# A message-passing layer on one core: three small moves in the order of work

## The chip, the cores and the metric

The kernel runs on one core of a Trainium2 chip. The metric is the device time of one execution in microseconds (us). Before the change the median of three runs is 1985.5 us (1981.94 to 1990.43). A separate execution was taken with the hardware profiler: 1976.44 us, of which 1974.5 us lie between the program's first and last instruction (the span). All views of the profile come from that one.

Engines: TensorE (PE, with its weight loads shown apart as PEld), VectorE (DVE), ScalarE (ACT), GpSimd (POOL) and SyncE (SP). SP, ACT and POOL also issue the DMAs, each on a queue of its own; an issuing instruction on SP or ACT is shown as SPq or ACTq.

## The reference

A graph has 12,500 nodes with 64 features each and 200,000 edges, sorted by target node. In short:

```python
nodes = x[edges].reshape(E, 128)                  # source row, target row
gates = ssp(edge_attr @ We1 + be1) @ We2 + be2    # ssp(v) = softplus(v) - log 2
gates = gates * (1 - sigmoid(5 * (dist - 3.5)))
h = ssp(nodes @ Wn1 + bn1) @ Wn2 + bn2
message_sum = zeros.at[edges[:, 1]].add(h * gates)
new = x + (ssp(message_sum @ Ws1 + bs1) @ Ws2 + bs2)
out = layernorm(x + new)
```

## The kernel before

**Groups and steps.** The edges are cut into 391 groups of 512, each of two halves of 256, and each half into two chunks of 128, so a group has four chunks. A loop over steps i (from -3, line 628) works on several groups at once: it transposes group i+3, runs layer 1 of group i+1, layer 2 of group i-1 and the scatter of group i-3. The order of instructions is written out by hand; each engine executes its own part of it in that order.

**What a group needs.** Source rows are gathered from x by POOL, one indirect DMA per chunk of 128 rows (line 230, tile xg), 14 groups ahead of the step, into 18 buffers. 40 chunks of all are instead fetched row by row with plain DMAs (line 250, tile xr), 17 of them on SP's queue and 23 on ACT's; `fetch` reads four scaled row numbers (a row number times 256 bytes) into registers first (line 244, tile rows_i). Edge features come by one SP transfer per group (line 268, tile eT, 128 partitions of 256 numbers, 7 buffers). Since the edges are sorted, the targets of a half lie in a window of 42 nodes. A table in DRAM holds, for each node, the target's part of layer 1; two SP transfers per group (line 275, tile wns) bring the windows of 42 table rows, with bases read into registers for two groups at a time (line 270). The chunk's one-hot of the target in its window is made by DVE (line 282).

**One step on PE**, in order: layer 2's bias into the PSUM tile gh (line 338, a product of three bf16 pieces, 512 columns), layer 2 of the edge features (342), layer 1's bias into the PSUM tile z (305, 256 columns), layer 1 of the edge features (307), layer 1 of the nodes (313, rows of xT against wns), the scatter (365), four transposes (296), and layer 2 of the nodes (348). There are two buffers each of z, gh and the transposes' tile. All waits of a step on transfers and on the one-hot are gathered on its first instruction, line 338, through `behind`; the list is

```python
needs = [("xcopy", i + 1), ("load", i + 1)]
needs += [(name, g) for g in ahead[i] for name in ("gather", "onehot")]
```

ACT then does the exponential (324), the logarithm (327) and the copy of the transposes (301); DVE does softplus (332), the products h and msg (357, 361) and the adding of windows into sums (382). About every 15 steps the sums of 512 nodes are complete and a node block (layers on the sums and the layer norm, lines 398 to 461) is strewn over the following steps. From step 380 on, the last ten groups run in a shorter pipeline (`ends`).

**The start.** Constants, indices and x are loaded; SP's queue carries, in this order, src_i, dst_h, three of seven parts of xT, rows_i, dist (tile cut), dst_l (tile rel), and later the other four parts of xT. ACT's queue carries the constants, Wn1 copied 14 times into wns (448 KB), then low_d, base_b, row_d and rows. low_d and base_b take the smallest target of each half through DRAM to all partitions; row_d and rows do the same for the biases in bf16 pieces (line 563, 565). ACT's next work behind them is copying the table's products from PSUM (578). DVE's first instruction is the scaling of the row numbers (492). After that the table stage (line 571 on) computes the table in 14 slices: PE multiplies, ACT and DVE copy, SP writes it to DRAM. Gathers of groups 5 to 13 are issued between the slices, each behind a small memset on DVE (223).

**DMA semaphores.** SP's and ACT's transfers (those of `fetch` aside) share eight semaphores, dealt out in turn in the order in which the program is laid down; a transfer waits until the last one on its semaphore has landed.

Of the kernel before, what the change touches and what calls it, by code (L numbers as in the profile page):

```python
# [42 lines left out]
F32 = mybir.dt.float32  # L43
# [4 lines left out]
OP = mybir.AluOpType  # L48
# [9 lines left out]
P = 128  # L58
D = 64
HE = 256  # L60
# [61 lines left out]
def gnn_resnorm_kernel(ctx: ExitStack, tc: tile.TileContext, a: dict, out: bass.AP, E: int):  # L122
    nc = tc.nc
    x = a["x"]
    N = x.shape[0]
    NG = a["eT"].shape[1]
# [12 lines left out]
    loads = ctx.enter_context(tc.tile_pool(name="loads", bufs=LOADS + 2))  # L139
# [3 lines left out]
    def z_tile():  # L143
        return psum.tile([P, 2, NB], F32, name="z")
# [34 lines left out]
    ones3 = const.tile([PIECES, HE], BF16, name="ones3")  # L179
    be3 = const.tile([PIECES, 2, D], BF16, name="be3")  # L180
    row3 = const.tile([PIECES, 2, K, D], BF16, name="row3")
# [3 lines left out]
    xgs, xrs, eTs = {}, {}, {}  # L185
    made = {}

    def note(key, ins):
        made.setdefault(key, []).append(ins)
        return ins  # L190

    def behind(ins, *keys):

        for key in keys:
            for other in made.get(key, []):
                tc.add_manual_dep(ins.ins, other.ins.name,
                                  mybir.DependencyInfo(mybir.DependencyClass.Sync, mybir.DependencyReason.DATA),
                                  reason="one place of a step takes its waits")
# [64 lines left out]
    bases = {}  # L263

    def load(g):
        eTs[g] = loads.tile([P, HE], F32, name="eT")
        old = ("scatter", g - LOADS - 2 - 4)
        behind(note(("load", g), nc.sync.dma_start(eTs[g], a["eT"][:, g, :])), old)  # L268
        if g % 2 == 0:
            _, at = nc.values_load_multi_w_load_instructions(  # L270
                base_i[32:33, 2 * g : 2 * g + 4], engines=[SP], min_val=0, max_val=8 * D * (N - 1),
                skip_runtime_bounds_check_because="they were clamped to these bounds")
            bases[g], bases[g + 1] = at[:2], at[2:]
        for h in range(2):
            behind(note(("load", g), nc.sync.dma_start(  # L275
                wns[D:DW, g % REST, h, :].bitcast(U8),
                table_bytes[:, bass.ds(bases[g][h], 8 * D * W)].rearrange("o (w f) -> (o w) f", w=W))), old)
# [21 lines left out]
    def xcopy(g):  # L299
        xT = work.tile([DW, K, P], F32, name="xT", bufs=3)  # L300
        note(("xcopy", g), nc.scalar.copy(xT, xTs[g]))  # L301
        xTs[g] = xT.rearrange("f (t h) e -> f h t e", h=2)

    def layer1_edge(g):
        nc.tensor.matmul(zs[g][:, 0, :HE], be3.rearrange("q h d -> q (h d)"), ones3, start=True, stop=False,  # L305
                         skip_group_check=True)
        nc.tensor.matmul(zs[g][:, 0, :HE], we1.rearrange("a h d -> a (h d)"), eTs[g], start=False, stop=True,  # L307
                         skip_group_check=True)

# [22 lines left out]
        nc.vector.scalar_tensor_tensor(ss[g].rearrange("p i t e -> p (i t e)")[:, part], us[g][:, part], BIG,  # L332
                                       z_of(g)[:, part], OP.min, OP.max)

    def layer2_edge(g, *needs):
        gh = gh_tile()
        v = gh.rearrange("p (i t h d) -> p i t h d", i=2, t=2, h=2)
        first = nc.tensor.matmul(gh, ones3[:, :P], row3.rearrange("q i k d -> q (i k d)"), start=True, stop=False,  # L338
                                 skip_group_check=True)
        behind(first, *needs)  # L340
        for t in range(2):
            nc.tensor.matmul(v[:, 0, t], ss[g][:, 0, t, :], we2, start=False, stop=False, skip_group_check=True)  # L342
        ghs[g] = gh.rearrange("p (i k d) -> p i k d", i=2, k=K)
# [128 lines left out]
    with tc.manual_schedule():  # L472
# [4 lines left out]
        with tc.tile_pool(name="prep", bufs=1) as prep:  # L477
# [11 lines left out]
            for i in range(3):  # L489
                load_x(i)  # L490
            nc.sync.dma_start(rows_i, a["rows"])
            nc.vector.tensor_scalar(rows_i, rows_i, float(4 * D), None, OP.mult)
            dist = cut.rearrange("p g k -> p (g k)")
            nc.sync.dma_start(dist, a["dist_l"])
            dst_i = rel.bitcast(I32)
# [75 lines left out]
            for i in range(PARTS):  # L571
                for c in range(i * CP, (i + 1) * CP, CP // 2):
                    m = CP // 2
                    ps = z_tile().rearrange("p b (k f) -> p (b k) f", k=K)
                    for k in range(m):
                        nc.tensor.matmul(ps[:, k, :], xT[:, c + k, :], wnb, start=True, stop=True)
                    tb = prep.tile([P, m, 2 * D], F32, name="tb", bufs=6)
                    nc.scalar.copy(tb[:, :K, :], ps[:, :K, :])
                    nc.vector.tensor_copy(tb[:, K:, :], ps[:, K:m, :])
                    nc.sync.dma_start(by_node[:, c : c + m], tb)  # L580
                    nc.vector.memset(sums[:, c * P : WIDE if c + m == NCH else (c + m) * P], 0.0)
                    for g in waiting.get(c // m, []):
                        gather(g, after=True)
                if i == 1:
                    nc.vector.tensor_copy(base_i[:1], base_b[:1])
                    nc.vector.tensor_scalar(base_i[32:33], base_b[32:33], float(8 * D), None, OP.mult)
                    for k in range(2):
                        nc.vector.tensor_copy(be3[:, k, :], rows[:, 0, :])
                    for k in range(K):
                        nc.vector.tensor_copy(row3[:, :, k, :], rows[:, 1:3, :])  # L590
                        nc.vector.tensor_copy(rs3[:, k, :], rows[:, 3, :])
                if i == 2:
                    nc.vector.tensor_scalar(dist, dist, CUTOFF - 1.5, 5.0, OP.subtract, OP.mult)
                    nc.scalar.activation(dist, dist, AF.Sigmoid)
                    nc.scalar.preload_act_table_set("natural_log_exp_and_others")
                    nc.vector.tensor_scalar(dist, dist, -1.0, 1.0, OP.mult, OP.add)
                    nc.vector.tensor_copy(rel, dst_i)
                    for t in range(2):
                        r = rel[:, :, 2 * t : 2 * t + 2]
                        nc.vector.tensor_sub(r, r, base_b[:, :NH].rearrange("p (g h) -> p g h", h=2))  # L600


        with tc.tile_pool(name="finish", bufs=1) as finish:
# [24 lines left out]
            for i in range(-3, last - 1):  # L628
# [7 lines left out]
                if i < ends:  # L636
                    needs = [("xcopy", i + 1), ("load", i + 1)]
                    needs += [(name, g) for g in ahead[i] for name in ("gather", "onehot")]
                    for g in second[i]:
                        layer2_edge(g, *needs)  # L640
                    if i >= -1:
                        zs[i + 1] = z_tile()
                        layer1_edge(i + 1)
                        for part in early:
                            part.tensor(tx_tile())
                    if i >= -1:
                        layer1_node(i + 1)
                    for n, g in enumerate(third[i]):
                        scatter(g, zs[i + 1][:, 1, HE + 2 * W * n : HE + 2 * W * (n + 1)])
                    at(exps, i + 1)  # L650
                    fetch(i, 1, 0, 0, ROWS // 2)
                    at(logs, i + 1)
                    fetch(i, 1, 0, ROWS // 2, ROWS // 2)
                    for g in ahead[i]:
                        transposes(g)
                        xcopy(g)
                    fetch(i, 1, 1)
                    for g in second[i]:
                        layer2_node(g)
                    for g in second[i]:  # L660
                        hcut(g)
                        message(g)
                    for g in third[i]:
                        window(g)
                    for part in early:
                        part.others()
                    at(softplus, i + 1)
                else:
                    for g in ahead[i]:
                        transposes(g)  # L670
                        xcopy(g)
                    zs[i + 1] = z_tile()
                    layer1_edge(i + 1)
                    for part in early:
                        part.tensor(zs[i + 1][:, 1, HE:])
                    layer1_node(i + 1)
                    exps(i + 1)
                    logs(i + 1)
                    for g in second[i]:
                        layer2(g)  # L680
                        hcut(g)
                        message(g)
                    softplus(i + 1)
                    for g in third[i]:
                        scatter(g, tx_tile()[:, : 2 * W])
                        window(g)
                    for part in early:
                        part.others()
# [19 lines left out]
            begun.pop(2).others()  # L708
            transposes(last)
            xcopy(last)  # L710
            zs[last] = z_tile()
            layer1_edge(last)
            layer1_node(last)
            for some in (edge, node):
# [177 lines left out]
```

## Time and profile before

| | |
|---|---|
| profiled execution | 1976.44 us, span 1974.5 us |
| median of three runs | 1985.5 us |
| PE busy | 1845.7 us (93%) |
| DVE busy | 1086.9 us (55%) |
| ACT busy | 922.5 us (47%) |
| POOL busy | 1447.6 us (73%), 1523 gathers |
| DMA engines, mean busy share in the loop | 0.28 |
| mean granted TensorE clock | 0.976 |

How to read the lines shown: in groups of instructions, a line has the source line, engine, operation, tile written <- tiles read, count | busy time in us, mean ns of one | idle time of the engine before them in us, and what ended it. In the timeline the columns are start, duration (us), engine, line, operation, tiles and count, and in brackets the idle time just before with what released the engine. In the tables by windows the columns are the window, its length, busy time and count on each engine, the granted clock, the DMA engines' busy share and GB/s. Matmuls are pipelined and their ends are modelled, so a busy PE need not be at its peak.

### The profile page before, as it was taken

The page shows a single profiled execution, that of the slowest core. Times are in us where ns is not written, and L with a number is a line of the kernel's source. Part 1 is how long each engine was busy: PE and PEld are TensorE (multiplying, and loading weights), DVE is VectorE, ACT ScalarE, POOL GpSimd, SP SyncE. Part 2 cuts the span into 40 slices and gives each one's busy share as a digit, 9 for nine tenths or more (in the row PEclk, how much of TensorE's full clock was granted, in tenths as well). Part 3 has the DMA queues.
Part 4 walks back from the last instruction along what each step waited for, and adds up shares of the span by engine and source line. Part 5 has one row for each costly group of instructions (what it writes and reads, how often), then busy time and mean ns, then how long its engine had stood idle before and what let it go on. Part 6 is the DMA issues. An engine that isn't in the chain of part 4 may idle for free.

```text
span 1974.5 us, 46877 instructions
## 1 busy us (share of the span) xinstructions
PE 1845.7 (93%) x11373; PEld 1532.7 (78%) x11373; DVE 1086.9 (55%) x2774; ACT 922.5 (47%) x1318; POOL 1447.6 (73%) x1527
## 2 busy tenths in 40 slices
PE   2899998999999999999999999999999999999996
PEld 2788877877777887778788787777877777878875
DVE  2555555555554565555555555565556555655664
ACT  0355544544444554444454544455444444544543
POOL 5777777777777777777777777777777777777771
PEclk9999999999998999999999999999999999999998
DMA  7422222222222222222222222222222323222320
GB/s 208 149 64 67 65 66 66 66 66 66 68 65 69 68 67 67 66 66 68 70 64 70 70 66 70 66 72 71 69 71 65 71 70 72 69 70 68 95 67 14
DMA packets 177321, 143.47 MB, mean 73 GB/s; under 512 B 53193, under 2 KB 149661, under 8 KB 177044
## 3 DMA queue, kind: packets, MB, share of 16 engines
q1 hardware_dynamic: 121052, 88.13, 15.5%
q0 software_dynamic: 48736, 50.00, 13.2%
q10 hardware_dynamic: 7256, 2.27, 0.6%
q8 instruction: 97, 1.59, 0.3%
q14 instruction: 180, 1.47, 0.3%
HBM read 130.59 MB, written 9.63 MB: 71 GB/s over the span
## 4 chain that ended last, share of the span: by engine, by line
PE 49%; SPq 30%; issue 9%; DMA 4%; DVE 2%; POOL 2%; ACTq 2%; ACT 1%; DVEq 0%; POOLq 0%
SPq L250 12%; PE z L313 10%; PE gh L348 8%; PE z L307 7%; PE gh L342 7%; SPq L275 6%; SPq L244 6%; PE tx L296 4%; PE z L365 4%; PE gh L338 3%; SPq L268 3%; POOL xg L230 2%; PE z L305 2%; SPq L270 2%; DMA wns<-table 2%
## 5 line engine op out<-in xcount | busy, mean ns | idle before, releaser
L230 POOL DMA_INDIRECT xg<-in_x,src_i x1523 | 1447.4, 950 | 483.8 <-issue 363.1
L324 ACT ACTIVATE u<-z 128x768 f32<-128x768 f32 x392 | 315.9, 806 | 626.6 <-PE z L365 417.9
L357 DVE TENSOR_TENSOR h<-gh,cut 128x256 f32<-128x256 f32 x391 | 165.9, 424 | 593.5 <-PE gh L348 577.2
L327 ACT ACTIVATE u<-u,one 128x768 f32<-128x768 f32 x392 | 365.9, 933 | 236.1 <-ACT u L324 229.2
L313 PE MATMUL z<-xT,wns 106*128 106x256 f32 x1564 | 419.9, 392 | 0.0
L332 DVE SCALAR_TENSOR_TENSOR s<-u,z 128x768 f32<-128x768 f32 x392 | 372.6, 951 | 77.4 <-ACT u L327 67.0
L348 PE MATMUL gh<-consts,s 128*128 128x64 f32 x3128 | 394.9, 270 | 0.0
L348 PEld LDWEIGHTS gh<-consts,s 128*128 128x128 f32 x3128 | 383.4, 193 | 0.1
L313 PEld LDWEIGHTS z<-xT,wns 106*128 106x128 f32 x1564 | 305.3, 197 | 46.3 <-ACT xT L301 0.9
L307 PE MATMUL z<-eT,consts 128*128 128x256 f32 x782 | 281.2, 442 | 0.0
L342 PE MATMUL gh<-consts,s 128*128 128x128 f32 x1564 | 280.7, 302 | 0.0
L342 PEld LDWEIGHTS gh<-consts,s 128*128 128x128 f32 x1564 | 205.6, 191 | 90.7 <-issue 89.9
L365 PEld LDWEIGHTS z<-xg,msg 128*128 128x128 f32 x1512 | 236.7, 198 | 22.2
L296 PE MATMUL tx<-consts,xg 128*106 128x128 f32 x1524 | 238.0, 277 | 4.0 <-DVE xg L282 2.7
L301 ACT COPY xT<-tx 106x512 f32<-106x512 f32 x391 | 221.6, 567 | 13.2 <-PE tx L296 13.0
L382 DVE TENSOR_TENSOR sums<-sums,z 64x42 f32 x756 | 148.7, 197 | 137.6 <-issue 56.2
L365 PE MATMUL z<-xg,msg 128*128 128x84 f32 x1512 | 223.0, 271 | 0.0
L338 PE MATMUL gh<-row,ones 3*128 3x512 bf16 x391 | 148.9, 381 | 71.8 <-DMA wns<-table 46.6
L296 PEld LDWEIGHTS tx<-consts,xg 128*106 128x106 f32 x1524 | 181.5, 144 | 5.1 <-DVE xg L282 3.0
L361 DVE TENSOR_TENSOR msg<-gh,h 128x256 f32<-128x256 f32 x391 | 165.8, 424 | 13.4
L307 PEld LDWEIGHTS z<-eT,consts 128*128 128x128 f32 x782 | 119.1, 192 | 47.8 <-issue 2.0
L282 DVE TENSOR_TENSOR xg<-consts,rel 128x168 f32<-128x168 f32 x391 | 128.7, 330 | 0.1
(103 smaller groups left out, 604.1 us busy)
## 6 DMA issues: line engine op xcount, KB each, us to landing
eT<-in_eT SPq DMA_DIRECT2D x391, 128.0 KB
xr<-in_x ACTq DMA_DIRECT2D x2944, 0.2 KB
xr<-in_x SPq DMA_DIRECT2D x2176, 0.2 KB
xg<-in_x,src_i POOLq DMA_INDIRECT x1523
wns<-table SPq DMA_DIRECT2D x782, 21.0 KB
table<-tb SPq DMA_DIRECT2D x14, 448.0 KB
sums<-in_xT SPq DMA_DIRECT2D x7, 455.0 KB
y<-in_x SPq DMA_DIRECT2D x24, 128.0 KB
```

The costliest lines, as they stand in the source:

```text
L230: note(("gather", g), nc.gpsimd.indirect_dma_start(out=xg[:, k, :D], out_offset=None, in_=x, in_offset=bass.IndirectOffsetOnAxis(ap=src_i[ ...
L250: ins = queues[queue].dma_start(row_tiles[n, "in"][r + j : r + j + 1, :D].bitcast(U8), x_bytes[:, bass.ds(row_at[queue][j], 4 * D)])
L296: nc.tensor.transpose(tx[:, k, :], xgs[g][:, k, :DW], ident)
L301: note(("xcopy", g), nc.scalar.copy(xT, xTs[g]))
L307: nc.tensor.matmul(zs[g][:, 0, :HE], we1.rearrange("a h d -> a (h d)"), eTs[g], start=False, stop=True, skip_group_check=True)
L313: nc.tensor.matmul(zn, wns[:, g % REST, h, :], xTs[g][:, h], start=True, stop=True, skip_group_check=True)
L324: nc.scalar.activation(us[g][:, part], z_of(g)[:, part], AF.Exp)
L327: nc.scalar.activation(us[g][:, part], us[g][:, part], AF.Ln, bias=one)
L332: nc.vector.scalar_tensor_tensor(ss[g].rearrange("p i t e -> p (i t e)")[:, part], us[g][:, part], BIG, z_of(g)[:, part], OP.min, OP.max)
L342: nc.tensor.matmul(v[:, 0, t], ss[g][:, 0, t, :], we2, start=False, stop=False, skip_group_check=True)
L348: nc.tensor.matmul(ghs[g][:, 1, 2 * t + h, :], ss[g][:, 1 + h, t, :], wn2, start=False, stop=h == 1 and t == 1, skip_group_check=True)
L365: ins = nc.tensor.matmul(sc, msgs[g][:, 2 * t : 2 * t + 2, :].rearrange("p h f -> p (h f)"), xgs[g][:, 2 * t : 2 * t + 2, D:DW], start=t = ...
```

## The change

Three things move. Layer 1's bias product is taken out of `layer1_edge` into `layer1_bias`; in the steps before the last ten it is issued first in the step, ahead of layer 2's bias, and takes the step's waits with it. Edge features of two groups come in one transfer, issued for the even one, into a tile of twice the size with four buffers. The scaling of the row numbers leaves the start of DVE's work and goes into the second part of the table stage.

```diff
     def load(g):
-        eTs[g] = loads.tile([P, HE], F32, name="eT")
         old = ("scatter", g - LOADS - 2 - 4)
-        behind(note(("load", g), nc.sync.dma_start(eTs[g], a["eT"][:, g, :])), old)
         if g % 2 == 0:
+            n = min(2, NG - g)
+            both = loads.tile([P, 2, HE], F32, name="eT", bufs=4)
+            behind(note(("load", g), nc.sync.dma_start(both[:, :n], a["eT"][:, g : g + n, :])), old)
+            for j in range(n):
+                eTs[g + j] = both[:, j]
             _, at = nc.values_load_multi_w_load_instructions(
...
+    def layer1_bias(g, *needs):
+        zs[g] = z_tile()
+        first = nc.tensor.matmul(zs[g][:, 0, :HE], be3.rearrange("q h d -> q (h d)"), ones3, start=True, stop=False,
+                                 skip_group_check=True)
+        behind(first, *needs)
+
     def layer1_edge(g):
-        nc.tensor.matmul(zs[g][:, 0, :HE], be3.rearrange("q h d -> q (h d)"), ones3, start=True, stop=False,
-                         skip_group_check=True)
...
-    def layer2_edge(g, *needs):
+    def layer2_edge(g):
...
-        first = nc.tensor.matmul(gh, ones3[:, :P], row3.rearrange("q i k d -> q (i k d)"), start=True, stop=False,
-                                 skip_group_check=True)
-        behind(first, *needs)
+        nc.tensor.matmul(gh, ones3[:, :P], row3.rearrange("q i k d -> q (i k d)"), start=True, stop=False,
+                         skip_group_check=True)
...
             nc.sync.dma_start(rows_i, a["rows"])
-            nc.vector.tensor_scalar(rows_i, rows_i, float(4 * D), None, OP.mult)
...
                     nc.vector.tensor_scalar(base_i[32:33], base_b[32:33], float(8 * D), None, OP.mult)
+                    nc.vector.tensor_scalar(rows_i, rows_i, float(4 * D), None, OP.mult)
...
+                    if i >= -1:
+                        layer1_bias(i + 1, *needs)
                     for g in second[i]:
-                        layer2_edge(g, *needs)
+                        layer2_edge(g)
                     if i >= -1:
-                        zs[i + 1] = z_tile()
                         layer1_edge(i + 1)
```

In the last ten steps `layer1_bias` stands directly ahead of `layer1_edge`, as the product did before.

More of the change, by code (lines that the diff above doesn't have):

```diff
@@ L671, in gnn_resnorm_kernel @@
                         xcopy(g)
-                    zs[i + 1] = z_tile()
+                    layer1_bias(i + 1)
                     layer1_edge(i + 1)
@@ L710, in gnn_resnorm_kernel @@
             xcopy(last)
-            zs[last] = z_tile()
+            layer1_bias(last)
             layer1_edge(last)
```

## The prediction

> **What bounds the kernel now.** I read the page first, then how far the gathers run ahead of PE (counts of two lines over growing windows), then SP's timeline in mid-run, the timeline of the first 45 us, and the last 80 us.
>
> The page's totals mislead: PE looks like the bound, POOL idle for a quarter of the time.
>
> ```profile
> PE 1845.7 (93%) x11373; PEld 1532.7 (78%) x11373; DVE 1086.9 (55%) x2774; ACT 922.5 (47%) x1318; POOL 1447.6 (73%) x1527
> L230 POOL DMA_INDIRECT xg<-in_x,src_i x1523 | 1447.4, 950 | 483.8 <-issue 363.1
> ```
>
> The idle time before a gather is "issue": 0.30 us after each, so a gather costs 0.95 + 0.30 = 1.25 us. 1523 of them are 1904 us, 4.87 us per group (391 groups). POOL waited for something only at the start (2.85 and 13.85 us), and it issues its last gather at 1930.75 us.
>
> Gathers issued (first fence) and layer 2 bias products, L338, one per step (second fence), from the start to 200, 1000 and 1895 us:
>
> ```profile
> 0.00:200.00 200.00, 137.11 (x142) 1.00 0.45 121
> 0.00:1000.00 1000.00, 742.29 (x780) 0.98 0.31 78
> 0.00:1895.00 1895.00, 1419.56 (x1494) 0.98 0.30 74
> ```
> ```profile
> 0.00:200.00 200.00, 9.39 (x25) 2.26 (x25) 1.00 0.45 121
> 0.00:1000.00 1000.00, 73.39 (x193) 17.50 (x193) 0.98 0.31 78
> 0.00:1895.00 1895.00, 143.87 (x378) 34.26 (x378) 0.98 0.30 74
> ```
>
> A group takes four gathers less the 40 chunks that SP and ACT fetch by rows (2, 20 and 40 of them by then), and step i needs group i+3. So at 200 us POOL has finished 36 groups and step 25 needs the 29th, a lead of 7; at 1000 us 200 against 197, a lead of 3; at 1895 us 383 against 382, a lead of 1. PE takes less per step than POOL, and its margin is used up just at the end. Group 382 (counting from 0) is gathered last at 1891.72; a gather lands 2.42 us after its start (chain of waits), at 1894.1; step 379, which needs it, starts at 1895.06. That is 0.9 us of room, and from there to the end PE is dense for 79 us.
>
> In mid-run PE is paced by SP's queue, two steps of which are:
>
> ```profile
> 499.85 1.24 SPq L250 DMA_DIRECT2D xr<-in_x  x4
> 501.19 0.37 SPq L268 DMA_DIRECT2D eT<-in_eT  x1
> 501.65 0.85 SPq L275 DMA_DIRECT2D wns<-table  x2
> 503.22 3.20 SPq L250 DMA_DIRECT2D xr<-in_x  x8
> 506.52 0.37 SPq L268 DMA_DIRECT2D eT<-in_eT  x1
> 507.54 0.78 SPq L275 DMA_DIRECT2D wns<-table  x2
> ```
>
> From 499.85 to the next such row at 509.09 is 9.24 us, 4.62 per step; the gaps between the rows are loads of bases and row numbers into registers (L270, L244), not waits. A node block's transfers come on top. PE idles before L338 for 71.8 us in all, 46.6 of them put down to wns. The chain names POOL around 240 to 340 us, but there POOL leads by about 6 groups: that is an attribution, not a limit.
>
> The start, timeline and waits:
>
> ```profile
> 20.43 0.22 DVE L492 TENSOR_SCALAR rows_i<-rows_i 40x128 int32<-40x128 int32 x1 [20.43 <-DMA rows_i<-in_rows]
> 25.00 0.30 ACTq L526 DMA_DIRECT2D low_d<-lowT  x1
> 26.21 1.57 SPq L487 DMA_DIRECT2D sums<-in_xT  x4
> 27.00 0.36 ACTq L528 DMA_DIRECT2D base_b<-low_d  x1
> 31.64 0.24 ACTq L563 DMA_DIRECT2D row_d<-pieces  x1
> 39.44 0.26 ACTq L565 DMA_DIRECT2D rows<-row_d  x1
> 43.09 0.06 DVE L223 MEMSET xg<- 128x1 f32 x1
> 43.42 0.94 POOL L230 DMA_INDIRECT xg<-in_x,src_i  x1 [13.85 <-DVE xg L223]
> ```
>
> DVE stands still for 20.43 us before the scaling of the row numbers, and all that follows on it waits: the bases (25.00), their round trip through DRAM, and at the end ACT, which can't copy the table's first products before row_d has landed (39.44). POOL's 13.85 us hang on that copy.
>
> **The change, part by part.**
>
> *Row numbers scaled later.* DVE's first wait becomes dst_h, issued at 1.70, ahead of rows_i (4.02). By 10 us the queues had moved 2.7 MB and dst_h ends at 1.7 MB of SP's, so I take about 9.5 us; the bounds are 4 and 16 us and matter little. DVE's chain from there to low_d (20.89 to 25.00, 4.1 us) then ends near 14, and the pieces near 20.5. But low_d goes out on ACT's queue behind wns (448 KB, issued 2.18, landed 26.2: SP's wait of 14.9 us on it ends at 26.21). A small transfer behind a large one on ACT's queue waits: row_d, 1.5 KB, took 7.8 us behind base_b. So the new limit is wns. The built order of the changed kernel shows that dist and rel (782 KB each) no longer compete with it: the eight DMA semaphores are dealt out in another order, dist now waits for wns, xT's sixth part for base_b. In the 6 us from 18 to 24 us, 289 GB/s moved 1.7 MB, nearly the size of those two, so wns could land at 20 at best, at 26.2 at worst; its rest is slow small packets, and I take 22.5. From wns's landing to base_b's issue is 0.8 us (26.21 to 27.00) and from there to row_d's landing 12.4 us (27.00 to 39.44), now beside dist and rel and two parts of xT rather than four parts: 8 to 14 us, kept at 12.4. Row_d lands at 22.5 + 0.8 + 12.4 = 35.7, **3.7 us earlier** (bounds 28.8 and 41.0: 10.6 earlier, 1.6 later). ACT's copies, L223 and POOL's restart move by the same. The multiply itself, 0.22 us, now stands before a tb copy on DVE: at most 0.2 us of PE's table stage, behind which POOL no longer waits. The first reader of the row numbers is ACT at 93.5 us.
>
> *Edge features in pairs.* 391 transfers become 196. Each removed one frees SP of its issue and wait, 0.46 us (501.19 to 501.65): SP's two steps shrink from 9.24 to 8.8 us, 4.4 per step. The 256 KB land in one piece, one step earlier than needed for the odd group; the queue rests at a DMA share of 0.28. Behind the removed wait comes the next: PE's own step, from the chain 0.32 + 0.64 + 0.21 + 0.63 + 0.86 + 0.41 + 0.44 + 0.85 = 4.36 us, with node blocks (about 2 us, 25 times) 4.49. Both are under POOL's 4.87. So PE eats its lead sooner and then waits for gathers, about 0.4 us a step. The gain here is the room at step 379: **0.9 us** (0 to 1).
>
> *Layer 1's bias first.* The same instructions in another order: L305 (0.21 us) goes ahead of L338 and L342. It carries the step's waits, plus z's release by softplus of two steps before. On DVE that softplus (L332) stands before the one-hot (L282), and a step waits for this one anyway, so nothing new ends last. Weight loads may overlap worse or better, 0.1 us a step either way; the 0.4 us of waiting for gathers covers it. Without that cover it would be 391 x 0.1 = 39 us. I take 0.
>
> Sum: 3.7 + 0.9 = 4.6 us off the profiled execution, from 1976.4 (span 1974.5 and 2 around it) to 1971.8. The median shown, 1985.5, lies 9.1 above that execution. If the surplus is late PE or SP work, the new slack swallows it; if it is slower gathers, none. I give a third, 3 us: 1985.5 - 4.6 - 3 = **1978**.
>
> [...] By stretches of 100 us the granted clock lay between 0.93 and 1.00, though PE idled at the fronts of steps by up to 2.7 us. [...]
>
> **Rivals.**
>
> 1. *The start does not move* (base_b slower beside dist and rel, or wns late). For it: all share the same 16 engines, at a share near 1.0 from 10 to 24 us. Against: 1.6 MB less beside wns. Then 0 to 4 us less than before: 1981 to 1985.
> 2. *POOL is no limit*, and SP's relief comes through: 46.6 to 71.8 us of PE's idle time go, 1985.5 - 4 - 47 to 72, so 1910 to 1934. Against it: 80 gathers in each 100 us, all run long.
> 3. *Slower: the wait at the front costs PE its clock.* PE's 4.49 us per step grow past POOL's 4.87 once the mean clock falls under 4.49/4.87 = 0.92. At 0.90 a step takes 4.99, and over the second 195 steps 0.12 x 195 = 23 us are lost: 2001. For it: the granted clock was 0.93 from 600 to 700 us, where PE had waited 1.7 us for wns (612.61, chain of waits). Against: the new waits are short and regular.
>
> **How the numbers follow.** Forecast 0.74 (times 1970 to 1986, by the bounds of the start and of the surplus), rival 1 0.12, rival 2 0.04, rival 3 0.10. The range 1968 to 1987 takes in the forecast and rival 1, less the far ends of the start, and leaves out the others. This kernel's runs can tell 0.5% from no change, 9.9 us. Faster than 1975.6: four tenths of the forecast, 0.29, and rival 2: 0.33. Slower than 1995.4: 0.09 of rival 3. Between: 0.58.
>
> **What would show it.** DVE's first wait ends by 12 us; the first copy of the table and POOL's restart near 39.5 instead of 43.4; SP's transfers of eT 196, with SP at times idle; L338's wait on wns nearly gone, and L305 now waiting for gathers; POOL still 80 gathers per 100 us, last one near 1927; the last gather to the end 43 us as before. The prediction is wrong if POOL's spacing changes, if wns still lands at 26, or if PE's clock falls under 0.92.

## The result and the profile after

The changed kernel takes 1968.63 us (median of five runs, 1964.49 to 1973.58) against 1985.71 (median of five, 1981.94 to 1990.43) for the kernel before: ratio 0.9915, 95% interval 0.9891 to 0.9939, 17.1 us less. The profiled execution takes 1968.45 us, of which 1966.5 are the span: 8.0 us less than before's profiled execution. The two are not of one kind: the changed kernel's is one of its five timed runs, before's is none of its five and lies 5.5 us under the fastest of them.

The page's busy times with its lines of the gathers and of the step's first product, now layer 1's bias (L309). Then, from tables by windows, the gathers counted from the start to 200, 1000 and 1888 us, and the products of L309, one per step, to 200 and 1888 (L309 works for group i+1, from step -1 on, so 29 of them is step 27, and 381 is step 379):

```profile
PE 1750.5 (89%) x11373; PEld 1491.4 (76%) x11373; DVE 1077.2 (55%) x2774; ACT 922.5 (47%) x1318; POOL 1445.0 (73%) x1527
L230 POOL DMA_INDIRECT xg<-in_x,src_i x1523 | 1444.8, 949 | 475.3 <-issue 319.4 <-DMA xg<-in_x,src_i 67.1 <-PE tx L299 31.1
L309 PE MATMUL z<-ones,be 3*128 3x256 bf16 x391 | 105.3, 269 | 167.8 <-DMA wns<-table 64.9 <-PE gh L354 29.2 <-DMA xg<-in_x,src_i 21.2
```
```profile
0.00:200.00 200.00, 143.37 (x148) 1.00 0.45 126
0.00:1000.00 1000.00, 748.32 (x788) 0.98 0.30 80
0.00:1888.00 1888.00, 1420.09 (x1497) 0.97 0.29 75
...
0.00:200.00 200.00, 7.79 (x29) 2.63 (x29) 1.00 0.45 126
...
0.00:1888.00 1888.00, 102.32 (x381) 34.52 (x381) 0.97 0.29 75
```

PE reaches step 27 by 200 us where it had reached step 25, so it uses up POOL's lead sooner, and its busy time falls by 95 us while its idle time grows. The gathers are as dense as before, eight more by 1000 us, and that is the head start from the beginning.

The start, in the same views as before's (timeline of DVE, SP, ACT and POOL):

```profile
9.87 1.09 DVE L523 CAST dst_h<-dst_h 128x1792 f32<-128x1792 int32 x1 [8.64 <-DMA dst_h<-in_dst_h]
20.50 0.28 DVE L565 CAST pieces<-brow 1x256 bf16<-1x256 f32 x1
...
21.91 0.36 SPq L499 DMA_DIRECT2D cut<-in_dist_l  x1
...
14.01 0.30 ACTq L531 DMA_DIRECT2D low_d<-lowT  x1
22.08 0.35 ACTq L533 DMA_DIRECT2D base_b<-low_d  x1
22.52 0.24 ACTq L568 DMA_DIRECT2D row_d<-pieces  x1
29.10 0.26 ACTq L570 DMA_DIRECT2D rows<-row_d  x1
...
33.07 0.94 POOL L230 DMA_INDIRECT xg<-in_x,src_i  x1 [4.30 <-DVE xg L223]
```

DVE starts at 9.87 us instead of 20.43. POOL restarts at 33.07 instead of 43.42, 10.35 us earlier. It issues its last gather at 1919.68 (timeline of POOL) against 1930.75: 11.07 earlier, of which 0.72 were gained on the way. The span's end is 8.0 earlier. So the last 46.8 us cost 3.1 more than before's last 43.75.

SP in mid-run, and what SP and PE wait for (waits; total, times, longest):

```profile
505.50 3.18 SPq L250 DMA_DIRECT2D xr<-in_x  x8
508.79 0.37 SPq L270 DMA_DIRECT2D eT<-in_eT  x1
...
514.25 3.18 SPq L250 DMA_DIRECT2D xr<-in_x  x8
```
```profile
SPq L278 <- PE z L371: 86.5, 51, 5.3
SPq L270 <- PE z L371: 48.3, 32, 4.9
```

Two steps of SP take 8.75 us (505.50 to 514.25) where they took 9.24. SP now waits for PE's scatter (L371), which frees the buffers that it fills: where it does, it is as far ahead as its buffers allow.

What PE waits for can be told by when the gathers start. A step needs the gathers of group i+3. The last of them for step 189 and the step's first product (timelines of POOL and PE):

```profile
955.19 0.94 POOL L230 DMA_INDIRECT xg<-in_x,src_i  x1 [0.30 <-issue]
958.17 0.26 PE L309 MATMUL z<-ones,be 3*128 3x256 bf16 x1 [1.08 <-DMA wns<-table]
```

The profile names wns, but the product starts 2.98 us after the gather's start, and so it goes on: of the 283 steps from 97 to 379, 272 start within 4.5 us of the start of their last gather, half of them within 2.97, and none sooner than 2.51. Of the 64.9 us that the page puts down to wns on L309, 53 end within 3.5 us of such a start; they are by all signs waits for gathers: the line carries both waits, and the profile names the one of several that it saw last. From step 97 (510 us) on PE follows POOL. In the kernel before, the same distance is 28.9 us at step 50, 14.3 at step 200 and 5.8 at step 359, and never under 3.29: its PE came near the gathers at the end, but did not wait for them.

### The profile page after: what moved, and what is told of

The parts are those of the page before. It is cut to its first block, busy times and chain, and to the rows that moved or that the text cites. A ratio compares the mean times of both kernels' runs of the same rounds, so it can differ in the third digit from the quotient of the medians.

```text
span 1966.5 us, 46634 instructions
## 1 busy us (share of the span) xinstructions
PE 1750.5 (89%) x11373; PEld 1491.4 (76%) x11373; DVE 1077.2 (55%) x2774; ACT 922.5 (47%) x1318; POOL 1445.0 (73%) x1527
## 4 chain that ended last, share of the span: by engine, by line
PE 46%; ACTq 14%; DMA 10%; SPq 10%; issue 9%; ACT 5%; DVE 3%; POOL 3%; DVEq 0%; POOLq 0%
ACTq L250 11%; PE z L320 10%; PE gh L348 7%; PE gh L354 6%; PE z L314 5%; PE z L371 5%; DMA xg<-in_x,src_i 4%; PE tx L299 4%; DMA wns<-table 4%; SPq L250 4%; ACT u L331 3%; ACTq L244 3%; PE z L309 3%; POOL xg L230 3%; PE gh L345 2%
## 5 line engine op out<-in xcount | busy, mean ns | idle before, releaser
L354 PE MATMUL gh<-consts,s 128*128 128x64 f32 x3128 | 395.7, 270 | 0.0
L354 PEld LDWEIGHTS gh<-consts,s 128*128 128x128 f32 x3128 | 384.7, 194 | 0.0
L371 PEld LDWEIGHTS z<-xg,msg 128*128 128x128 f32 x1512 | 237.9, 199 | 22.9
L309 PE MATMUL z<-ones,be 3*128 3x256 bf16 x391 | 105.3, 269 | 167.8 <-DMA wns<-table 64.9
L314 PE MATMUL z<-eT,consts 128*128 128x256 f32 x782 | 242.4, 393 | 0.0
L371 PE MATMUL z<-xg,msg 128*128 128x84 f32 x1512 | 223.3, 271 | 0.0
L309 PEld LDWEIGHTS <-be 3*128 3x128 bf16 x391 | 35.4, 91 | 206.6 <-issue 102.9
```

Of the source, the lines that this page charges most:

```text
L354: nc.tensor.matmul(ghs[g][:, 1, 2 * t + h, :], ss[g][:, 1 + h, t, :], wn2, start=False, stop=h == 1 and t == 1, skip_group_check=True)
L371: ins = nc.tensor.matmul(sc, msgs[g][:, 2 * t : 2 * t + 2, :].rearrange("p h f -> p (h f)"), xgs[g][:, 2 * t : 2 * t + 2, D:DW], start=t = ...
```

## The experiments

All four groups of experiments ran on chips (1, 15, 6 and 12) on which the kernel before takes 2510 to 2562 us with a recorded TensorE clock near 0.85, so their ratios are to the kernel before on the same chip. The record names no chip for the first comparison; that it ran on another is read from its time. It is called the first chip below. What sets the end where it takes 1986 us was thus never tried by a run. The start takes its 45 us on every chip, and could be.

### The parts alone, and two changes of POOL's work

**Rows alone:** the kernel before with one line moved.

```diff
             nc.sync.dma_start(rows_i, a["rows"])
-            nc.vector.tensor_scalar(rows_i, rows_i, float(4 * D), None, OP.mult)
...
                     nc.vector.tensor_scalar(base_i[32:33], base_b[32:33], float(8 * D), None, OP.mult)
+                    nc.vector.tensor_scalar(rows_i, rows_i, float(4 * D), None, OP.mult)
```

> The kernel before with the scaling of the row numbers moved alone; edge features still one transfer per group, layer 1's bias in its old place. Theory P (the end hangs on POOL's gathers, and POOL restarts 10 us earlier): the restart of the gathers falls from 43.4 to about 33 us as in the changed kernel, POOL's last gather to about 1920, and the median to about 1976, 10 us below before. What is then missing to the changed kernel's 1968.6, about 7 us, is lateness on SP's and PE's side that only the pairs remove. Theory S (the rows' scaling is small, SP's relief is the gain): 3 to 5 us below before, 1981 or more.

Measured: 2549.64 against 2562.26, ratio 0.9952 (0.9935 to 0.9969).

**Pairs alone:** the kernel before with the new `load`.

> The kernel before with edge features in pairs alone. Theory P: POOL's restart stays at 43.4 us and its last gather at 1931; the median falls by what late PE and SP work added to the runs of before, 0 to 7 us, so 1979 to 1986; SP's wait on PE's scatter appears and PE waits for gathers from about group 100 on. Theory S: 10 to 17 us below before, 1969 to 1976, with the last gather still at 1931 but PE's end earlier.

Measured: 2529.16 against 2562.26, ratio 0.9868 (0.9849 to 0.9888).

**Eight gathers more** in the changed kernel:

```diff
+            if k == 0 and 40 <= g < 360 and g % 40 == 0:
+                spare = loads.tile([P, D], F32, name="spare", bufs=8)
+                nc.gpsimd.indirect_dma_start(
+                    out=spare, out_offset=None, in_=x,
+                    in_offset=bass.IndirectOffsetOnAxis(ap=src_i[:, g, k : k + 1], axis=0))
```

> The changed kernel with eight gathers more, of groups 40 to 320, into a spare tile that nobody reads; nothing waits for them. Theory P: each costs POOL 1.25 us and nothing else hides it: 10 us above the changed kernel, about 1978.6, ratio to before 0.996. A rival that sets the end by PE or SP: under 2 us above the changed kernel, about 1969, ratio 0.9915.

Measured: 2525.09, ratio 0.9847 (0.9830 to 0.9864).

**One group more gathered ahead of the table stage** in the changed kernel: `FREE = 5` becomes `FREE = 6`.

> The changed kernel with the gathers of one group more (six instead of five) issued ahead of the table stage, so that POOL doesn't wait 4.3 us for the first slice of the table (28.8 to 33.1 us). Theory P: POOL goes on without a hole, its last gather moves from 1920.6 to about 1916.5, and the median to about 1964.5, 4 us under the changed kernel. A rival that sets the end by PE or SP: no change, 1968.6.

Measured: 2521.59, ratio 0.9852 (0.9832 to 0.9873).

The order is the reverse of what I expected: the pairs are worth 33 us, the rows 12.6. The last two kernels should lie 14 us apart by POOL's work, and their ratios of 0.9847 and 0.9852 lie within each other's intervals, so on this chip POOL is not the limit. (The changed kernel itself was not run on it.) The rows' 12.6 us are near what the start gains; the lines below show it twice. The expected times were written for a chip like the first and are of no use here; that gathers count for nothing does tell something, and it leaves the theory that POOL sets the end without an experiment of its own.

### The start, and what lies beside base_b

**Without the rows' part** (pairs and bias) and **without the pairs** (rows and bias):

> The changed kernel with the scaling of the row numbers put back to its old place: pairs and the earlier bias product alone. Theory P on a chip with the kernel before at 1986 us: the restart of POOL is back near 43.4 us, and only the room of up to 1 us at the last gathers is left, so 1983 to 1987 us, ratio 0.998 to 1.001. Rival (SP's relief moves the end): a ratio of 0.995 or less without the earlier start. On the chip where the kernel before takes 2562 us, pairs alone gave 0.9868; the bias first adds nothing by my account, so the same within 0.002; a rival that the bias product hides the wait for wns gives 0.980.

> The changed kernel without the pairs: one transfer of edge features per group again; the rows' scaling and the earlier bias product stay. Theory P on a chip with the kernel before at 1986 us: POOL restarts near 33 us, 10 us earlier, and the whole gain is there: 1969 to 1976 us, ratio 0.991 to 0.995, since PE is still ahead of POOL at the end (lead of one group before), or, where SP's 9.24 us per two steps no longer keep up with a POOL that is 10 us further, only part of it: PE averaged 4.87 us per step over the run and its lead is used up, so up to 9 us of the 10 would be lost, ratio 0.999. On the chip where the kernel before takes 2562 us: the rows alone gave 0.9952; the same within 0.002 if the bias is worth nothing.

Measured against 2510.15: without the rows' part 2476.54, ratio 0.9864 (0.9817 to 0.9910); without the pairs 2498.95, ratio 0.9947 (0.9918 to 0.9976). Beside the parts alone (0.9868 and 0.9952), the bias product is worth 0.0005 or less in either, which is nothing that these intervals, up to 0.005 to each side and taken on two chips, can tell. The theory's part on this chip (pairs alone and the same with the bias) came out; the rival of 0.980 did not.

The start of both (timelines of ACT and POOL), first with the row numbers scaled first as in the kernel before, then with them scaled later:

```profile
26.84 0.36 ACTq L534 DMA_DIRECT2D base_b<-low_d  x1
32.01 0.24 ACTq L569 DMA_DIRECT2D row_d<-pieces  x1
39.12 0.26 ACTq L571 DMA_DIRECT2D rows<-row_d  x1
...
43.10 0.94 POOL L230 DMA_INDIRECT xg<-in_x,src_i  x1 [13.16 <-DVE xg L223]
```
```profile
22.53 0.35 ACTq L530 DMA_DIRECT2D base_b<-low_d  x1
22.97 0.24 ACTq L565 DMA_DIRECT2D row_d<-pieces  x1
29.40 0.26 ACTq L567 DMA_DIRECT2D rows<-row_d  x1
...
33.37 0.94 POOL L230 DMA_INDIRECT xg<-in_x,src_i  x1 [4.87 <-DVE xg L223]
```

They agree within 0.6 us with the two kernels of the first comparison. In all eleven kernels profiled that scale the row numbers late, row_d has landed between 27.2 and 30.5 us; in the three that scale them first, between 39.1 and 39.4. So the start's 10 us come from the row numbers alone on these chips, and the first chip's lines are the same. The span from base_b's issue to the end of row_d is 12.3 us in the first of these two and 6.9 in the second.

Why it shrank was the question, and my first thought was the traffic: before, four late parts of xT went out beside base_b; after, dist and dst_l do. **dist and dst_l behind the late parts of xT:**

```diff
             nc.sync.dma_start(rows_i, a["rows"])
-            dist = cut.rearrange("p g k -> p (g k)")
-            nc.sync.dma_start(dist, a["dist_l"])
-            dst_i = rel.bitcast(I32)
-            nc.sync.dma_start(dst_i.rearrange("p g k -> p (g k)"), a["dst_l"])
...
             for i in range(3, PARTS):
                 load_x(i)
+            dist = cut.rearrange("p g k -> p (g k)")
+            nc.sync.dma_start(dist, a["dist_l"])
+            dst_i = rel.bitcast(I32)
+            nc.sync.dma_start(dst_i.rearrange("p g k -> p (g k)"), a["dst_l"])
```

> The changed kernel with one edit: the transfers of dist and dst_l (782 KB each) stand behind the four late parts of xT instead of ahead of them. The four parts of xT (65 partitions each) then go out beside base_b, as they did in the kernel before, while everything else of the change stays. Theory N (what lies on the queues beside base_b sets how fast base_b and row_d land): base_b is issued near 22 us as in the changed kernel, but from there to the table's first copy it takes about 12.4 us again as before, so the copy comes near 34.5 us and POOL restarts near 38, 5 us later than in the changed kernel; the time is about 5 us above it. Rival V (an earlier start or fewer bytes made base_b fast, not its neighbours): four xT parts are 1.8 MB against 2.0 to 2.5 MB of dist, dst_l and one or two xT parts, so the copy comes at 29 us or sooner, and the time is that of the changed kernel. The start can be read on either of the two chips; on the one where the kernel before takes 2562 us the total should hardly show 5 us.

Measured: 2463.3 against 2510.15, ratio 0.9820 (0.9774 to 0.9866). SP's and ACT's timelines:

```profile
21.94 1.71 SPq L493 DMA_DIRECT2D sums<-in_xT  x4
26.42 0.36 SPq L570 DMA_DIRECT2D cut<-in_dist_l  x1
...
21.69 0.35 ACTq L529 DMA_DIRECT2D base_b<-low_d  x1
22.29 0.24 ACTq L564 DMA_DIRECT2D row_d<-pieces  x1
28.11 0.26 ACTq L566 DMA_DIRECT2D rows<-row_d  x1
```

All four parts of xT leave within 2 us of base_b, as in the kernel before, and row_d has landed 6.4 us after base_b's issue. (dist now stands fifth behind rows_i, in the place of xT's sixth part, whose semaphore is base_b's: in the changed kernel SP waits 5.0 us for base_b there; it leaves at 26.42, so base_b took under 4.8 us, if the order of the semaphores holds.) Theory N, that the neighbours on the queues slowed base_b and row_d, falls: the table's first copy starts at 29.69 where it asked for about 34.5. The ratio, 0.9820 beside 0.9818 of the changed kernel on chip 12, would agree, but could hardly tell 5 us. What did it is in the chain of waits through the start:

```profile
4.02 16.39 DMA rows_i<-in_rows
...
31.33 0.29 DVE pieces L560
31.64 7.78 DMA row_d<-pieces
```
```profile
14.01 8.05 DMA low_d<-lowT
22.08 6.77 DMA base_b<-low_d
28.86 0.50 DMA sums<-in_xT
29.39 1.28 ACT L583
```

The first is the kernel before, the second the changed one. Before, base_b was not on the path: row_d was issued at 31.64 because DVE finished the last of the bias pieces at 31.62. The 12.4 us from base_b to row_d were 4.64 of DVE's work and 7.80 of transfer. After, DVE has the pieces at 20.78 while the queue still waits for wns and low_d, row_d goes out 0.44 after base_b, and the transfer takes 6.58.

### What sets the pace on the slower chips

**SP fetches no rows**; POOL gathers its 17 chunks, so the edit also gives POOL 17 gathers more.

```diff
-    return max(0, 2 * i + 2 if queue else (3 * i + 4) // 2)
+    return max(0, 2 * i + 2 if queue else 0)
```

> The changed kernel, but SP fetches no rows: its 17 chunks are gathered by POOL instead, which is 17 gathers more by 1.25 us, 21 us of POOL, and 2176 transfers less on SP's queue. Where POOL sets the end (theory P, a chip with the kernel before at 1986 us): the last gather is issued 21 us later, near 1941 us, and the time is near 1990 us, 1.0 to 1.1% above the changed kernel, slightly slower than the kernel before (ratio 1.00). Rival Q (SP's queue still sets the pace there): the time falls by some tens of us instead. On the chip where the kernel before takes 2562 us: theory S (SP's queue sets the pace there, since its instructions stand still for 0.7 us at a time): the time falls to what POOL and PE need, 1990 to 2100 us, ratio 0.78 to 0.82; the rival (PE's clock of 0.85 sets the pace there): it stays at 2500, ratio 0.98.

Measured: 2508.37 against 2510.15, ratio 0.9989 (0.9956 to 1.0023). Both accounts for such a chip are wrong: taking 2176 transfers off SP's queue and giving POOL 17 gathers does not speed the kernel up, it takes away the whole gain. So SP's queue alone does not set the pace there, and relief of SP may not be all of the reason why the pairs are worth 1.3%. Where the gain went, some 45 us (0.9989 against 0.9820 of the kernel with dist last on the same chip), is not known: eight gathers more cost nothing, 17 were not tried alone.

**Both bias products left out**, so a step has 0.53 us less of PE:

```diff
-        first = nc.tensor.matmul(zs[g][:, 0, :HE], be3.rearrange("q h d -> q (h d)"), ones3, start=True, stop=False,
-                                 skip_group_check=True)
-        behind(first, *needs)
+        first_needs[g] = needs
...
-        nc.tensor.matmul(zs[g][:, 0, :HE], we1.rearrange("a h d -> a (h d)"), eTs[g], start=False, stop=True,
-                         skip_group_check=True)
+        first = nc.tensor.matmul(zs[g][:, 0, :HE], we1.rearrange("a h d -> a (h d)"), eTs[g], start=True, stop=True,
+                                 skip_group_check=True)
+        behind(first, *first_needs[g])
...
-        nc.tensor.matmul(gh, ones3[:, :P], row3.rearrange("q i k d -> q (i k d)"), start=True, stop=False,
-                         skip_group_check=True)
...
```

The other products of layer 2 then start their sums themselves; the output lacks these biases.

> The changed kernel with both bias products of a step left out (the one of layer 1 and the one of layer 2; the output lacks these biases): PE's step loses 0.21 + 0.32 = 0.53 us of its 4.36, 391 x 0.53 = 207 us of PE in all, and nothing else changes. Theory P on a chip with the kernel before at 1986 us: POOL sets the end, so only the dense tail after the last gather gets shorter, some 18 steps x 0.53 = 10 us: 1959 us, ratio 0.986. The rival there (PE sets the pace): 1760 to 1800 us. On the chips where the kernel before takes 2510 to 2560 us: theory C (PE's true speed sets the pace there, lower than the granted clock tells): 12% of the steps' time, 2150 to 2250 us, ratio 0.86 to 0.90; the rival (SP, POOL or the transfers): within 2% of the changed kernel on the same chip.

**The changed kernel beside it:**

> The changed kernel once more, beside the run without bias products. On a chip with the kernel before at 1986 us: ratio 0.9915 as before. On one where the kernel before takes 2510 to 2560 us: the parts measured there multiply to 0.9868 x 0.9955 = 0.982 if they add up; a ratio above 0.987 would say that they share one cause.

Measured against 2514.41: without bias products 2472.16, ratio 0.9820 (0.9782 to 0.9858); the changed kernel 2466.15, ratio 0.9818 (0.9789 to 0.9847). The parts add up (0.982). And 782 products fewer on PE, 12% of a step by the first chip's durations, change nothing. Theory C falls in the form in which it was put.

What is different on these chips can be seen in the waits: ACT and DVE wait for something that the profile calls "remote", an update for which it finds no instruction that ended near it. Neither kernel of the first comparison has such a wait. POOL has it too: in the changed kernel it stands 285.2 us in 203 such waits before its gathers, so it is held back there. First the two largest waits of the changed kernel on its slower chip, then, from the kernel without SP's rows, a stretch of the timeline:

```profile
ACT u L331 <- remote: 556.9, 198, 9.6
DVE h L363 <- remote: 511.5, 207, 15.3
```
```profile
1197.64 1.00 PE L354 MATMUL gh<-consts,s 128*128 128x64 f32 x8
...
1207.36 0.42 DVE L363 TENSOR_TENSOR h<-gh,cut 128x256 f32<-128x256 f32 x1 [11.01 <-remote]
```

DVE's product h needs gh, whose last product (L354) is recorded as done at 1198.64; DVE is let go at 1207.36. So on these chips PE seems to finish later than its records say, while the granted clock stood at 1.0 up to 1206; no run here shows what held it in these 8.7 us. What sets the pace on these chips stays open: ten us more of gathers, 2176 fewer transfers of SP and 782 fewer products of PE did not move it the way that a limit there would.

### Two kernels on another chip

Eight gathers more and rows alone, on chip 6:

> The changed kernel with eight gathers more on POOL (into tiles that nobody reads), 8 x 1.25 = 10 us of POOL, run once more in the hope of a chip like that of the first comparison. Theory P (POOL sets the end) on a chip with the kernel before at 1986 us: the last gather and the end come 10 us later than in the changed kernel, 1979 us, ratio 0.996 to 0.998. Rival (PE or SP sets the end): as the changed kernel, 1969, ratio 0.991. On chips where the kernel before takes 2510 to 2560 us it gave 0.985 and should again: the gathers do not count there.

> The kernel before with the scaling of the row numbers moved and nothing else. Theory P on a chip with the kernel before at 1986 us: POOL restarts 10 us earlier and the end follows as far as SP and PE keep up, 1972 to 1978 us, ratio 0.993 to 0.996; the rival, that SP's queue holds PE back once POOL is 10 us ahead, gives 0.998 to 1.000. On chips where the kernel before takes 2510 to 2560 us: 0.995 as on the first such chip.

Measured against 2513.96: 2466.78, ratio 0.9807 (0.9774 to 0.9840), and 2504.58, ratio 0.9956 (0.9936 to 0.9977). A slower chip too. The rows' worth repeats (0.9952, 0.9956); the changed kernel with ten us more of POOL is again no slower than the changed kernel, whose ratio of 0.9818 is from chip 12.

## Why the prediction was right or wrong

**What held.** The forecast was 1978 with a range of 1968 to 1987, and the case was the forecast's: POOL restarts earlier, the same dense gathers follow, and the end moves. That the time lies in the range is in good part luck. 1968.63 is 0.6 above its lower edge and below the 1970 that the forecast's own bounds gave; the gain of 17.1 us is more than twice the 7.5 forecast. The start and the surplus were both taken too small, and the tail, taken as unchanged, cost 3.1. Step by step:

- *DVE's first wait*: taken as 9.5 us, measured 9.87. Low_d "near 14": 14.01. Pieces "near 20.5": 20.50 for the last one's start. Wns at 22.5: SP's wait on it ended at 21.91.
- *SP's two steps*: 8.8 us expected, 8.75 measured, and SP idles as expected, waiting for PE.
- *Bias first*: taken as zero, and nothing speaks against it. The two pairs of kernels with and without it differ by 0.0005 or less on the other chips, with intervals up to ten times that. Its cover on the first chip was not tried.
- *PE uses up its lead and then waits for gathers*: it does from step 97 on. Layer 2's bias product comes 9.2 us earlier than before at step 1, 25.3 at step 90 and 10.1 at step 379. The first is the start; PE then gained 16 us more on its own, which fits SP's shorter steps, and the gathers took them back. On the first chip POOL's last gather moved by 11.07 us and PE's work after it followed by 10.5 until 1939 us. So POOL sets the pace to the end in the changed kernel. That is a reading of two traces, and no experiment stands behind it, since none ran on such a chip.

**What failed: the 12.4 us from base_b to row_d.** I kept the span whole and put it behind wns: 35.7. It landed at 29.10. The same paragraph has the pieces ready at 20.5; carried through, row_d's issue was 23.3 + 0.4 and its landing 23.7 + 7.8 = 31.5. The span was measured between two instructions of ACT's queue, but the second waited for DVE, and DVE's work was just what the change moved. The lower bound, 28.8 for row_d, was close: 10.6 us earlier was its price, 10.35 came. My reason for a faster or slower transfer, the neighbours, was put to a run, and with xT's parts back in their place the span stayed at 6.4 us.

**What failed: the 0.9 us of room and the tail's 43 us.** The room did not close: step 379 starts 4.10 us behind the start of its last gather (1880.77 to 1884.87), where it had been 3.34 (1891.72 to 1895.06). And the tail cost 3.1 us more. PE waits 2.01 us for DVE there in both traces. Before, it stays at full clock; after, it stands at half from about 1939 on for 6.8 us. Tables by windows (window, length, PE's busy time and count, granted clock, DMA share, GB/s) and two lines of PE's timeline, first of the kernel before:

```profile
1945.00:1949.50 4.50, 2.49 (x13) 1.00 0.10 29
1949.50:1952.50 3.00, 3.00 (x24) 1.00 0.00 0
```
```profile
1947.41 0.74 PE L432 MATMUL z<-consts,l_s 128*128 128x128 f32 x4 [2.01 <-DVE l_s L424]
1953.45 0.38 PE L338 MATMUL gh<-row,ones 3*128 3x512 bf16 x1
```

and then of the changed one:

```profile
1935.00:1939.00 4.00, 2.09 (x11) 1.00 0.11 33
1939.00:1942.00 3.00, 3.00 (x16) 0.50 0.00 0
1942.00:1945.80 3.80, 3.80 (x13) 0.50 0.00 0
```
```profile
1936.91 0.74 PE L438 MATMUL z<-consts,l_s 128*128 128x128 f32 x4 [2.01 <-DVE l_s L430]
1946.06 0.39 PE L345 MATMUL gh<-row,ones 3*128 3x512 bf16 x1
```

POOL's last gather is 11.07 us ahead of before; PE is 10.5 ahead at the product behind the wait, 7.39 at the next step's bias, and 8.0 at the end. So 0.6 are lost ahead of the wait, 3.1 at half clock, and 0.6 are regained behind it. The same wait, 2.01 us of idle PE, cost nothing in one execution and was followed by the loss of 3.1 us in the other; two executions do not show the cause. My forecast charged nothing for the clock behind the waits at the fronts of steps, and no run shows how long a wait has to be to cost it. The mean clock fell only from 0.976 to 0.970, far from the 0.92 at which rival 3 decides, so charging nothing held in size.

**The surplus.** I gave 3 of the 9.1 us by which the timed median lay above the profiled execution. With the medians of the second comparison it was 9.3 us before and 0.2 after. The profiled executions differ by 8.0 us, 3.4 more than the 4.6 worked out; the timed ones by 17.1. The gap between forecast and result, 9.4 us, is thus 3.4 of the traces and 6 of the surplus. Whether a surplus went at all is not shown. The 0.2 compares five runs with one of them, the 9.3 compares five with a sixth that was faster than all of them, so before's profiled execution may just have been a fast one. The pairs' relief of SP, which the other chips pay for with 33 us, would be another candidate. So the traces account for 8.0 of the 17.1 us, and the other 9.1 stay open.

**The rivals.** Rival 1 (the start does not move) is out: row_d landed 10.3 us earlier. Rival 3 (PE loses its clock) needs a mean clock under 0.92; it was 0.970. Rival 2 (POOL is no limit) is wrong on the first chip, by its price, 1910 to 1934, and by the distances above; but it describes the other chips, as far as tried: ten us of gathers cost nothing on two of them, and the pairs bring 1.3% on two.

## What to carry to other kernels

A span between two issues on one queue is not a transfer time: ask of the second one what it waited for, and where that was another engine's work which the change moves, take the two apart; the chain of waits shows it. Where one instruction carries several waits, the name that the profile gives is weak evidence: measure the distance to the start of each candidate, as for the gathers here. Work that stands first on an engine because its data were expected early can hold everything behind it: a 0.22 us multiply behind a 16 us load cost 10 us at the start, of which 8.0 were left at the end in the first chip's two traces. And which part of a change pays can turn over from chip to chip: rows 0.5% and pairs 1.3% where the kernel takes 2510 to 2562 us, while on the first chip the traces have the start behind what they show of the gain.

## What the runs showed of the hardware

The same program takes 1986 us in the first comparison and 2510 to 2562 us on the four chips of the experiments, with a recorded mean clock of 0.976 (profiled kernel before) against 0.85 (kernels of these experiments), and on those chips the time did not follow PE's instructions: 782 products of 11373 fewer left it the same (ratio 0.9820 against 0.9818) at a recorded clock of 0.827 against 0.861. A transfer of 3.5 KB behind one of 448 KB on ACT's queue took 8.05 us to land (low_d behind wns), and one of 1.5 KB behind base_b 4.9 to 8.0 us in the eleven kernels that scale late, 5.8 with four parts of xT beside it and the rest with dist and dst_l. And 2.01 us of idle PE were followed by 6.8 us at half clock in one execution, from 2 us behind the wait's end on, and by none in the other.
